# A fused attention, mixture-of-experts and rotation kernel: skew stores in six bundles, at most two scatters under way, and other places for some VectorE work

## The chip, the cores and the metric

The kernel runs on one core of a Trainium2 chip. The metric is the device time of one execution in microseconds (us); nine runs of the kernel before gave 685.74 to 692.51 us, median 689.94 us. All arithmetic is 32-bit floating point.

## The reference, cut to what matters

The input x has 4 batches of 512 tokens of 288 numbers. With a modulation computed from a condition vector, the reference computes, in this order:

```
h = ln(x) * (1 + scale) + shift                  # first half: attention
q, k, v = h @ w_qkv ; 16 heads of 18
x = x + gate * (softmax(q k^T / sqrt(18)) v @ w_proj)
xn = ln(x) * (1 + scale2) + shift2               # second half: experts
two of four experts per token, chosen by xn @ w_gate, gates by softmax
x = x + gate2 * sum(gate_e * (gelu(xn @ w1[e] + b1[e]) @ w2[e] + b2[e]))
v = silu(cond) @ W.T + b                         # 2016 numbers per batch
A = the 64x64 skew matrix with v above its diagonal and -v below ; R = expm(A)
U = Q of the QR factorization of P (288 x 64)
x = x + (z R - z) U^T   with z = x U
```

So beside the two large parts there are three small serial computations: the skew matrix and its exponential, the QR factorization (Householder, 64 columns one after the other), and the routing of tokens to experts.

## The kernel before, in words

The order of the work on each engine is written out by hand: each engine, and each DMA queue, executes its instructions strictly in the order in which the program issues them. What is said below of "before" and "behind" is this order.

**Attention.** 16 groups (4 batches b of 4 groups of four heads; group number n = 4b + g), each of four steps (128 keys each), so 64 steps, taken as 32 pairs numbered 0 to 31; a batch is 8 pairs, batch b begins at pair 8b. A step is `weigh`, that is 4 score matmuls (L1825) into a two-buffer PSUM tile z and two exponentials on ScalarE (L1834), and `gather`, 4 matmuls (L1845) of the exponentials with the values. The scores of a step can only be issued when the exponentials of the step before have emptied z. A pair p runs in this order:

1. `weigh(2p+1)`,
2. the pieces of its slot "a", then of slot "s",
3. one piece of the list `beside` (called "mid" below),
4. `weigh(2p+2)`, `gather(2p)`, `gather(2p+1)`; where a group ends: copy of its sums to oraw (ScalarE, L1864) and four small loads of the softmax denominators, den (L1867, SyncE's queue),
5. the pieces of slot "b", then another piece of `beside` (called "end"),
6. on GpSimd's queue: two stores that clear the slots, and up to five scatters.

The pieces that the change touches or moves things past:

- `reciprocals(n)` (slot "s"): VectorE inverts den (L1873), SyncE's queue stores it (rdr, L1875) and loads it back spread over the heads (spread, L1880). `divide(n)` (L1886, VectorE): oraw times spread. For group 3 of batch b these stand in pairs 8b+8 and 8b+9.
- `merge(b)` (pairs 8b+10 and 8b+11, slot "s"): four tiles of the output projection po (L1911), each of which reads all four oraw of the batch; VectorE adds po to xs (L1919) and takes its statistics (L1165).
- `begin(b+1)`: `first`, the layer norm's statistics of the next batch on VectorE (L1165, L1166) and four GpSimd operations behind them (L1178 to L1184); `norm`, four ScalarE activations with them (L1193), in slot "a" of pair 8b+2, so between the exponentials of two steps; `turns` and `values`, transposes and the value projection (L1214, L1736).
- `column` (L1585): one Householder column of the QR factorization, some 20 VectorE instructions that touch nothing else; 22 of them run in attention, the others in the expert part.
- `skew_matrices` (L1301): `product` (mid of pair 6) computes the 2016 numbers into four partition bands `row` of 504; `stores` writes them to a DRAM image of the matrices, one DMA for each run of a matrix row in a band, 66 in all; `load` reads the image, `last` transposes and subtracts. Four pieces of `stores` follow `product`, one for each band; the bands hold 9, 11, 14 and 32 runs.
- `rotations` (L1393): the exponential of A, 17 pieces called norm, levels, three powers, four Horner steps, turn, six squarings, last; `exponentials` puts empty pieces between them. TensorE does small products, VectorE the rest.
- `route` and `choose`: logits, top two, ranks, and at pair 23, slot "b", `slots_of`, the addresses where the tokens go. Then 16 scatters (L2178), one for 128 tokens and one choice, write the rows of the first half of the tokens into DRAM; up to five are issued at each pair's end. `slots_load` (pair 28) waits for all of them and loads the first expert's rows, xg (L2242 to L2249), on GpSimd's queue; TensorE transposes them in pairs 30 and 31 (L2293). The other 16 scatters follow in the expert part, one for each piece of expert work.

**Experts.** Eight expert halves one after the other: 36 weight tiles each for the hidden layer (L2531, L2544) and the output layer (L2591); the rest of the QR columns run on VectorE beside them. Then the rotation is applied and stored.

Of the kernel before, what the change touches and what calls it, by code (L numbers as in the profile page):

```python
# [20 lines left out]
HQ = 32  # L21
# [792 lines left out]
def fast_path(  # L814
# [24 lines left out]
    nc = tc.nc  # L839
    B, N, C = x.shape  # L840
# [4 lines left out]
    NG = w_qk.shape[2] // P  # L845
# [3 lines left out]
    D = pT.shape[0]  # L849
# [106 lines left out]
    with ExitStack() as s1:  # L956
# [344 lines left out]
        def skew_matrices(between):  # L1301

            width = NV // 4
            right.close()
            skew = right.enter_context(tc.tile_pool(name="skew", bufs=1, side="right"))
            um = skew.tile([2 * D, BH, D], F32, name="um")
            udr = dram.tile([D, B, D], F32, name="udr")
            wr = skew.tile([CC, NK, NV], F32, name="wr")  # L1310
            brs = skew.tile([P, width], F32, name="brs")
            row = brs

            def loads():
                nc.gpsimd.memset(um, 0.0)
                for h in range(2):
                    nc.gpsimd.dma_start(
                        out=udr[:, ts(h, BH), :], in_=um[ts(h, D), :, :]
                    )
                nc.gpsimd.memset(brs, 0.0)  # L1320
                for i in range(4):
                    nc.gpsimd.dma_start(
                        out=brs[i * HQ : i * HQ + B, :],
                        in_=br[ts(i, width)].partition_broadcast(B),
                    )
                for i in range(4):
                    nc.gpsimd.dma_start(
                        out=wr[:, :, ts(i, width)],
                        in_=wrT[:, ts(i, width)].rearrange("(k p) f -> p k f", p=CC),
                    )  # L1330

            def product():
                pa = bank([P, N], "pa")
                for k in range(NK):
                    for i in range(4):
                        nc.tensor.matmul(
                            pa[ts(i, HQ), :width],
                            scp[:, k, :],
                            wr[:, k, ts(i, width)],
                            start=(k == 0),  # L1340
                            stop=(k == NK - 1),
                        )
                nc.vector.tensor_add(row, pa[:, :width], brs)

            def stores(i, half):
                at, count = 0, 0
                for r in range(D - 1):
                    n = D - 1 - r
                    lo, hi = max(at, i * width), min(at + n, (i + 1) * width)
                    count += lo < hi  # L1350
                    if lo < hi and count % 2 == half:
                        nc.sync.dma_start(
                            out=udr[r, :, ds(r + 1 + lo - at, hi - lo)],
                            in_=row[i * HQ : i * HQ + B, ds(lo - i * width, hi - lo)],
                        )
                    at += n

            def load():
                for h in range(2):
                    nc.sync.dma_start(out=um[ts(h, D), :, :], in_=udr[:, ts(h, BH), :])  # L1360

            def last():
                pt = bank([P, N], "ptA")
                for b in range(BH):
                    for h in range(2):
                        at = ts(h, D)
                        nc.tensor.matmul(
                            pt[at, ts(b, D)],
                            um[at, b, :],
                            ident[at, at],  # L1370
                            start=True,
                            stop=True,
                        )
                nc.vector.tensor_sub(
                    A.rearrange("p b d -> p (b d)"),
                    um.rearrange("p b d -> p (b d)"),
                    pt[:, : BH * D],
                )
                right.close()

            idle = [lambda: None]
            return (
                [loads]
                + between
                + idle * 5
                + [product]
                + [lambda i=i: (stores(i, 0), stores(i, 1)) for i in range(4)]
                + [load]
                + idle * 5
                + [last]  # L1390
            )

# [569 lines left out]
        def choose(b, xr):  # L1962
# [190 lines left out]
            def slots_of():  # L2153
# [23 lines left out]
                def scatter(t, i):  # L2177
                    made = nc.gpsimd.indirect_dma_start(  # L2178
                        out=slots[h],
                        out_offset=bass.IndirectOffsetOnAxis(  # L2180
                            ap=where[:, i, t : t + 1], axis=0
                        ),
                        in_=xrs[t // NT][:, t % NT, :],
                        in_offset=None,
                        bounds_check=SLOTS - 1,
                        oob_is_err=False,
                    )
                    tc.declare_no_dep(
                        made.ins,
                        group=f"scatters{h}",  # L2190
                        reason="rows of one scatter are in no other",
                    )
                    tc.add_to_no_dep_group(f"scatters{h}", made.ins)
                    scattered[h].append(made.ins)

                scatters.extend(
# [111 lines left out]
        def exponentials():  # L2308
            pieces = []
            for i, piece in enumerate(rotations()):  # L2310
                pieces += [piece] + [lambda: None] * (3 if i == 0 else 1 + int(i == 1) if i < 11 else 0)
            pieces.pop(0)()
            beside[:0] = pieces[1:]

# [21 lines left out]
        def also(pair, slot, *pieces):  # L2336
            plan[pair][slot].extend(pieces)
# [7 lines left out]
        def divide(n):  # L2345
            ends_of[n][1]()
# [24 lines left out]
        for b in range(B):  # L2371
            at = b * HALF
            last = b == B - 1

            for p in {1: (0, 1, 6), 2: (0, 1, 7), 3: range(6)}.get(b, range(8)):
                also(at + p, "a", column)

            if b:
# [28 lines left out]
            for g in range(NG):  # L2407
                n = NG * b + g
                also_at = at + 2 * g + 2
                if also_at < PAIRS:  # L2410
                    also(also_at, "s", lambda n=n: reciprocals(n))
                    also(also_at + 1, "b", lambda n=n: divide(n))

            also(at + (4 if 0 < b < B - 1 else 6), "a", lambda b=b: residual(b))
            for p in {1: (3,), 2: (3,), 3: (6,)}.get(b, ()):
                also(at + p, "b", column)
            if not last:
                first, norm, turns, values = begin(b + 1)
                also(at + 1, "a" if b else "b", first)
                also(at + 2, "a" if b else "b", norm)  # L2420
                also(at + 3, "s", *turns)
                also(at + 4, "s", *values[:2])
# [501 lines left out]
```

## Time and profile before

The profiled execution took 689.83 us; the span of its instructions is 688.1 us, so 1.7 us lie around it.

| engine | busy us | share of the span |
|---|---|---|
| TensorE matmul (PE) | 660.6 | 96% |
| TensorE weight load (PEld) | 394.8 | 57% |
| VectorE (DVE) | 485.5 | 71% |
| ScalarE (ACT) | 294.5 | 43% |
| GpSimd (POOL) | 228.8 | 33% |

| part of the span | from us | to us |
|---|---|---|
| before the first exponential | 0 | 27.6 |
| attention, pairs 0 to 31 | 27.6 | 296 |
| experts and rotation | 296 | 688.1 |

How to read it: a line of the timeline gives start, duration, engine, source line, operation, the tiles written and read, and in brackets the idle time before it and what ended that. A line of the waits gives who waited for whom, the total, the number of times and the longest. A line of the stretches gives, for each engine, busy time and number of instructions, then the TensorE clock that was granted (1.00 is full speed), the DMA engines' busy share and GB/s. "SPq" is SyncE's queue. A matmul of 32-bit numbers shows as two records. A busy share of TensorE is not its peak: records of matmuls that follow each other slowly also look busy.

### The profile page before, as it was taken

The page shows a single profiled execution, that of the slowest core. Times are in us where ns is not written, and L with a number is a line of the kernel's source. Part 1 is how long each engine was busy: PE and PEld are TensorE (multiplying, and loading weights), DVE is VectorE, ACT ScalarE, POOL GpSimd, SP SyncE. Part 2 cuts the span into 40 slices and gives each one's busy share as a digit, 9 for nine tenths or more (in the row PEclk, how much of TensorE's full clock was granted, in tenths as well). Part 3 has the DMA queues.
Part 4 walks back from the last instruction along what each step waited for, and adds up shares of the span by engine and source line. Part 5 has one row for each costly group of instructions (what it writes and reads, how often), then busy time and mean ns, then how long its engine had stood idle before and what let it go on. Part 6 is the DMA issues. An engine that isn't in the chain of part 4 may idle for free. (4 is left out here: it accounts for less than half of the span.)

```text
span 688.1 us, 11454 instructions
## 1 busy us (share of the span) xinstructions
PE 660.6 (96%) x3563; PEld 394.8 (57%) x3563; DVE 485.5 (71%) x2207; ACT 294.5 (43%) x468; POOL 228.8 (33%) x352
## 2 busy tenths in 40 slices
PE   6999996999999999999999999999999999999995
PEld 5534333533353434356776767777677676776763
DVE  4554985397769888775996888888888887052135
ACT  4468564664566556751444223222232322312232
POOL 4034833415354277440431572304014032140110
PEclk9999998997999999999999999999999999999998
DMA  9457522212322124633631553344353053532035
GB/s 213 112 168 198 153 48 60 75 54 67 97 61 70 48 90 139 164 107 71 199 79 31 203 151 120 113 117 132 67 173 82 9 186 74 163 115 68 13 124 173
DMA packets 70624, 75.47 MB, mean 110 GB/s; under 512 B 33548, under 2 KB 57842, under 8 KB 70554
## 3 DMA queue, kind: packets, MB, share of 16 engines
q1 hardware_dynamic: 60166, 47.78, 25.7%
q0 software_dynamic: 9888, 26.45, 12.6%
q8 instruction: 30, 0.49, 0.3%
q10 hardware_dynamic: 500, 0.42, 0.3%
q14 instruction: 40, 0.33, 0.2%
HBM read 52.13 MB, written 18.23 MB: 102 GB/s over the span
## 5 line engine op out<-in xcount | busy, mean ns | idle before, releaser
L2591 PE MATMUL pe<-w2s,hm 128*128 128x288 f32 (+1 forms) x648 | 163.8, 408 | 0.0
L2531 PE MATMUL ph<-xgT,w1s 128*128 128x288 f32 (+2 forms) x576 | 151.7, 413 | 0.4
L1834 ACT ACTIVATE es<-z 128x1024 f32<-128x1024 f32 x128 | 126.2, 1022 | 58.1 <-PE z L1825 56.8
L2591 PEld LDWEIGHTS pe<-w2s,hm 128*128 128x128 f32 (+1 forms) x648 | 118.6, 187 | 32.0 <-issue 2.8
L2531 PEld LDWEIGHTS ph<-xgT,w1s 128*128 128x128 f32 x576 | 105.9, 190 | 40.2 <-issue 11.4
L2553 ACT ACTIVATE hm<-ph,b1r 128x576 f32<-128x576 f32 (+2 forms) x72 | 49.8, 737 | 132.5 <-PE ph L2544 132.5
L1825 PE MATMUL z<-qk 32*128 32x512 f32 x512 | 86.6, 648 | 1.3 <-ACT es L1834 1.3
L2606 POOL TENSOR_TENSOR y<-y,gb 128x288 f32<-128x288 f32 x32 | 27.7, 864 | 144.7 <-ACT y L2605 144.7
L1845 PE MATMUL av<-es,vt 128*32 128x512 f32 x512 | 62.3, 603 | 0.0
L2605 ACT ACTIVATE y<-pe,weight 128x288 f32<-128x288 f32 x32 | 16.0, 500 | 102.7 <-PE pe L2591 102.7
L1785 PE MATMUL pq<-hT,wqk 96*126 96x512 f32 (+3 forms) x120 | 55.7, 605 | 0.0
L2607 POOL DMA_INDIRECT chosen<-y,place x36 | 37.6, 1043 | 50.6 <-DVE y L2603 36.5
L1583 DVE SCALAR_TENSOR_TENSOR q<-q 64x1 f32<-64x1 f32 (+1 forms) x192 | 48.4, 252 | 6.9
L1825 PEld LDWEIGHTS z<-qk 32*128 32x128 f32 x512 | 28.6, 184 | 40.0 <-ACT es L1834 27.2
L2178 POOL DMA_INDIRECT slots<-xr,where x32 | 32.3, 1008 | 35.2 <-DVE where L2175 26.1
L1911 PE MATMUL po<-wpg,oraw 128*128 128x288 f32 x128 | 37.6, 442 | 6.6 <-POOL rs L1178 5.4
L1594 DVE STREAM_SHUFFLE wj<-pt 32x288 f32<-32x288 f32 (+47 forms) x96 | 42.1, 438 | 0.7
L1797 POOL DMA_DIRECT2D qk<-row x42 | 21.2, 513 | 58.2 <-ACT row L1792 57.9
L1785 PEld LDWEIGHTS pq<-hT,wqk 96*126 96x126 f32 (+3 forms) x120 | 20.4, 181 | 33.4 <-issue 30.2
L1845 PEld LDWEIGHTS av<-es,vt 128*32 128x32 f32 x512 | 13.6, 110 | 44.0 <-issue 44.0
L1911 PEld LDWEIGHTS po<-wpg,oraw 128*128 128x128 f32 x128 | 25.1, 204 | 21.2 <-issue 7.0
L1565 DVE SCALAR_TENSOR_TENSOR pt<-wj,uf,pt 64x288 f32<-64x288 f32 (+62 forms) x63 | 32.5, 515 | 2.2
(280 smaller groups left out, 869.1 us busy)
## 6 DMA issues: line engine op xcount, KB each, us to landing
w2s<-in_w_dram SPq DMA_DIRECT2D x8, 1296.0 KB
w1s<-in_w_dram SPq DMA_DIRECT2D x8, 1152.0 KB
slots<-empty POOLq DMA_DIRECT2D x36, 148.0 KB, 2.4
spread<-rdr SPq DMA_DIRECT2D x64, 64.0 KB
qk<-row POOLq DMA_DIRECT2D x42, 72.0 KB, 2.7
yc<-chosen SPq DMA_DIRECT2D x4, 576.0 KB
out_dram<-xs SPq DMA_DIRECT2D x8, 288.0 KB
wr<-in_wrT_dram POOLq DMA_DIRECT2D x4, 567.0 KB, 6.6
```

The source lines that it names most:

```text
L1565: nc.vector.scalar_tensor_tensor(m, w, u[rows, :], m, ALU.mult, ALU.add)
L1583: nc.vector.scalar_tensor_tensor(s, u, part, s, ALU.mult, ALU.add)
L1594: nc.vector.stream_shuffle(wj[o : o + HQ, j:], pt[o0 : o0 + HQ, j:], [j % HQ] * HQ)
L1785: nc.tensor.matmul(pq[:n], wqk[:rows, k, item, :n], hT[:rows, k, :], start=(k == 0), stop=(k == NK - 1),)
L1825: nc.tensor.matmul(zs[c // 2][:, c % 2, :], qk[ts(c, HQ), 1, ts(t, P)], qk[ts(c, HQ), 0, :], start=True, stop=True,)
L1834: nc.scalar.activation(e, z, AF.Exp, scale=SCALE)
L1845: nc.tensor.matmul(avs[n][ts(c, HQ), :], vts[b % 2][:, t, ds((4 * g + c) * (HD + 1), HQ)], es[c // 2][:, c % 2, :], start=(t == 0), stop=( ...
L1911: nc.tensor.matmul(po, oTs[NG * b + g][:, ts(t, P)], wpgs[b][:, g, :], start=(g == 0), stop=(g == NG - 1),)
L2531: nc.tensor.matmul(ph[:, j, :SB], w1s[:, k, ts(f, P)], xgT[:, k, ts(j, SB)], start=(k == 0), stop=False,)
L2553: nc.scalar.activation(hm[:, f, : CAPS[r]].rearrange("p (j s) -> p j s", j=NB), ph[:, :, :SB], AF.Gelu_apprx_tanh, bias=b1r[:, h, r, f : f ...
L2591: nc.tensor.matmul(po[ts(m, rows), :], slots_[:, f, :], w[:, f, :], start=(f == 0), stop=(f == NF - 1),)
L2607: nc.gpsimd.indirect_dma_start(out=chosen[h], out_offset=bass.IndirectOffsetOnAxis(ap=place[:, t : t + 1], axis=0), in_=y, in_offset=None, ...
```

## The change

- The 66 runs of the skew vector are put in one list in the order of the matrix's rows, and every sixth of it makes a bundle: six pieces of 11 stores in place of four of 9, 11, 14 and 32. One of the five empty pieces behind `load` goes, so `last` and the exponential's pieces come one piece (half a pair) later; one empty piece behind the first squaring goes too, so that from the second squaring on all stands where it stood.
- A scatter waits until the scatter two before it has landed. Before, no scatter waited for another.
- `divide` of a batch's last group moves from slot "b" to slot "s" of pair 8b+9.
- `column` moves from slot "a" to slot "b" in pairs 8, 9, 16, 17, 24 and 25.
- `first` of batches 2 and 3 moves from slot "a" to slot "b" of pairs 9 and 17, where it stands behind that pair's column.

```diff
-            def stores(i, half):
-                at, count = 0, 0
-                for r in range(D - 1):
-                    n = D - 1 - r
+            runs, at = [], 0
+            for r in range(D - 1):
+                n = D - 1 - r
+                for i in range(at // width, (at + n - 1) // width + 1):
                     lo, hi = max(at, i * width), min(at + n, (i + 1) * width)
-                    count += lo < hi
-                    if lo < hi and count % 2 == half:
-                        nc.sync.dma_start(
-                            out=udr[r, :, ds(r + 1 + lo - at, hi - lo)],
-                            in_=row[i * HQ : i * HQ + B, ds(lo - i * width, hi - lo)],
-                        )
-                    at += n
+                    runs.append((r, r + 1 + lo - at, i, lo - i * width, hi - lo))
+                at += n
+
+            def stores(part):
+                for r, to, i, lo, n in runs[part::6]:
+                    nc.sync.dma_start(
+                        out=udr[r, :, ds(to, n)],
+                        in_=row[i * HQ : i * HQ + B, ds(lo, n)],
+                    )
...
                 + [product]
-                + [lambda i=i: (stores(i, 0), stores(i, 1)) for i in range(4)]
+                + [lambda part=part: stores(part) for part in range(6)]
                 + [load]
-                + idle * 5
+                + idle * 4
                 + [last]
...
-                    tc.declare_no_dep(
-                        made.ins,
-                        group=f"scatters{h}",
-                        reason="rows of one scatter are in no other",
-                    )
-                    tc.add_to_no_dep_group(f"scatters{h}", made.ins)
+                    if scattered[h]:
+                        tc.declare_no_dep(
+                            made.ins,
+                            scattered[h][-1],
+                            reason="rows of one scatter are in no other",
+                        )
+                    if len(scattered[h]) > 1:
+                        tc.add_manual_dep(
+                            made.ins,
+                            scattered[h][-2].name,
+                            mybir.DependencyInfo(
+                                mybir.DependencyClass.Sync,
+                                mybir.DependencyReason.DATA,
+                            ),
+                            reason="two scatters at a time",
+                        )
...
-                pieces += [piece] + [lambda: None] * (3 if i == 0 else 1 + int(i == 1) if i < 11 else 0)
+                pieces += [piece] + [lambda: None] * (3 if i == 0 else 1 + int(i == 1) if i < 10 else 0)
...
-            for p in {1: (0, 1, 6), 2: (0, 1, 7), 3: range(6)}.get(b, range(8)):
+            for p in {1: (6,), 2: (7,), 3: range(2, 6)}.get(b, range(8)):
                 also(at + p, "a", column)
...
-                    also(also_at + 1, "b", lambda n=n: divide(n))
+                    also(also_at + 1, "s" if g == NG - 1 else "b", lambda n=n: divide(n))
...
-            for p in {1: (3,), 2: (3,), 3: (6,)}.get(b, ()):
+            for p in {1: (0, 1, 3), 2: (0, 1, 3), 3: (0, 1, 6)}.get(b, ()):
                 also(at + p, "b", column)
             if not last:
                 first, norm, turns, values = begin(b + 1)
-                also(at + 1, "a" if b else "b", first)
+                also(at + 1, "b", first)
                 also(at + 2, "a" if b else "b", norm)
```

## The prediction

> **What bounds the kernel now.** I read the page first: TensorE shows 96% busy, and from 296 us on every slice is full, so the experts pass on whatever attention gains or loses, one for one. The chain of waits covers only the last 24 us and names nothing here. So I looked at attention by stretches, one for each pair, and compared pairs of the same content in batches 1 and 2:
>
> ```profile
> core 0: us, PE busy (x) PEld busy (x) DVE busy (x) ACT busy (x) POOL busy (x), PEclk, DMA share, GB/s
> 105.60:124.20 18.60, 13.40 (x60) 7.55 (x56) 11.40 (x46) 6.58 (x9) 6.51 (x12) 0.82 0.22 63
> 186.20:197.00 10.80, 10.60 (x60) 5.70 (x58) 7.72 (x27) 6.59 (x9) 6.02 (x12) 1.00 0.21 59
> 213.20:222.10 8.90, 7.52 (x50) 2.68 (x46) 8.49 (x35) 4.49 (x5) 0.46 (x1) 1.00 0.22 66
> 156.00:168.10 12.10, 11.00 (x40) 5.68 (x44) 10.95 (x54) 4.80 (x7) 8.83 (x15) 0.62 0.30 93
> 229.70:239.70 10.00, 8.79 (x70) 4.73 (x66) 8.96 (x50) 4.72 (x6) 3.49 (x7) 1.00 0.31 81
> ```
>
> These are pairs 10, 18, 21, 15 and 23. Pair 10 costs 7.8 us more than its twin 18, pair 15 costs 2.1 more than 23, and both show a TensorE clock below 1. Then the waits of batch 1 (88.8 to 168.1 us):
>
> ```profile
> ACT xh L1193 <- POOL ms L1184: 6.9, 1, 6.9
> PE po L1911 <- POOL rs L1178: 5.2, 1, 5.2
> DVE den L1873 <- DMA udr<-brs: 4.4, 1, 4.4
> ACT g L2022 <- DVE g L2018: 3.5, 1, 3.5
> ```
>
> The second has a wrong name: `po` reads oraw, and `divide(3)` ended at 115.47 us, just before it resumed at 115.61. The queue of SyncE tells why `divide(3)` was late:
>
> ```profile
> 93.80 6.71 SPq L1352 DMA_DIRECT2D udr<-brs  x20
> 100.61 2.42 SPq L1867 DMA_DIRECT2D den<-oraw  x4
> 103.13 5.50 SPq L1352 DMA_DIRECT2D udr<-brs  x14
> 108.73 0.35 SPq L1875 DMA_DIRECT2D rdr<-den  x1
> 110.16 1.69 SPq L1880 DMA_DIRECT2D spread<-rdr  x4
> 111.95 10.76 SPq L1352 DMA_DIRECT2D udr<-brs  x32
> 124.33 1.14 SPq L1360 DMA_DIRECT2D um<-udr  x2
> 125.51 2.49 SPq L1867 DMA_DIRECT2D den<-oraw  x4
> ```
>
> The denominators stand behind skew stores at 0.336 us each. The clock, in two stretches:
>
> ```profile
> 115.60:121.30 5.70, 5.69 (x12) 4.13 (x13) 1.54 (x4) 2.18 (x4) 5.20 (x10) 0.50 0.20 53
> 158.90:169.10 10.20, 10.20 (x38) 5.29 (x40) 9.28 (x43) 3.30 (x5) 6.34 (x11) 0.50 0.29 93
> ```
>
> Half speed follows TensorE's idle 5.2 us (from 110.4, while `po` waited) and, the second time, an idle 1.35 us at 155.75.
>
> **The change part by part.** All sums are against the profiled 689.83 us (688.1 span, 1.7 around it), 0.11 below the median shown.
>
> *Stores.* The total stays 66 x 0.336 = 22 us of SyncE's queue. Ahead of group 3's den stand 22 stores in place of 20: den at 101.3, and den inverted 5.9 us later as before, at 107.1 (106.47 before). Behind it 11 in place of 14: the store of rdr no longer waits for the queue, spread goes out at 108.9 and lands 3.6 us later (as 130.88 to 134.46 did), at 112.5. The bundle of 32 becomes three of 11, with nothing between the first two and den of group 4 behind all: it goes out at about 121.6, not 125.51.
>
> *Columns, division, statistics in pairs 8 to 10.* Before, VectorE did column 8 (5.6 us) from 96.45 while den was on its way, and idled 4.4. After, it idles from 96.45 to 107.1, does column 8 (5.54) to 113.0, divides at once, and `po` resumes 0.83 us later, at 113.8: TensorE's wait is 3.4, not 5.2. But now column 9 stands ahead of the statistics: 113.7 + 5.5 + 2.34 = 121.6 (114.75 before). GpSimd's four operations take 2.55 more, ScalarE's norm 2.18: the exponentials of step 22 queued behind it start at 126.4, not 124.21. The next scores (step 23) need the first of them, 1.02 us: 127.5 against 125.90. **+1.6 us** for all of attention. The cover of the late statistics, TensorE's `po` until 123, is used up.
>
> *The clock after it.* TensorE has 4.6 us of `po` (18 records in pair 18), then 1.1 and 1.9 of scores and gathers, and idles from about 122 to 127.5. The bounds: no half speed, 0; half speed as after the 5.2 us, where those 18 records took 7.43 in place of 4.60 us, +2.8. The idle is nearest to that row: **+2.8**.
>
> [...]
>
> *Pairs 11 to 15.* Den of group 4 is inverted at about 126, not 129.17; its spread lands at 131.2. `divide(4)` then waits for the fourth `po` tile: 132.4 to 135 (134.46 before). From there to the top-two weights VectorE is full, 134.46 to 155.25 = 20.8 us: 153.2 to 155.8. ScalarE comes to `ratio` at 151.93 + 1.6 or + 4.4 = 153.5 or 156.3. So the wait of 3.5 us there goes, TensorE's 1.35, and the half speed behind them (the value projection took 6.13 us in place of 3.18 in pair 7). Late next: `levels`, now mid of pair 14 behind that pair's column. Its An, which the first power (end of pair 15) needs: weights + choices 1.1, divide 0.7, column 5.5, gates 1.0, reciprocals 0.45, levels 3.65 = 165.6 to 168.2. TensorE gets there at about 164 or 167. So the scores of step 33, at 170.34 before, come at 166.9 to 169.6: **-5.1** beside the +4.4, net -0.7 (-3.4 at full clock).
>
> *Pair 18.* Same reordering, statistics end at about 192.9 (190.35), norm at 197.6; the scores of step 39 came at 198.74 behind gathers, and the first exponential ends at 198.6: **0**, without slack; +0.5 if it slips.
>
> *Rotation pieces, half a pair later.* The third Horner product's wait for VectorE (1.38 us, pair 21) and the first squaring's (1.22, pair 23) go; `turn`, at the end of pair 22, waits for the last Horner step, which stands behind the top-two and a division: bounds -2.6 and 0, taken **-1.0**. Pieces from the second squaring on do not move. Columns 24 and 25 go behind small squarings that wait for nothing: 0; +0.4 if one squaring is late.
>
> *Scatters.* GpSimd is never idle over 0.31 us from `slots_of` to the last scatter, and the first expert's rows come right behind it:
>
> ```profile
> 273.48 0.97 POOL L2178 DMA_INDIRECT slots<-xr,where  x1 [0.31 <-issue]
> 276.64 0.95 POOL L2242 DMA_DIRECT2D xg<-slots  x1 [2.19 <-issue]
> 277.58 3.50 POOL L2245 DMA_DIRECT2D xg<-slots  x4
> ```
>
> These loads land 6.6 us (median) after issue, the last at about 287, and TensorE transposes them at 287.74: no slack. A scatter starts every 1.28 us and lands after 2.5/2.5/4.2 us (min, median, max), so the one two before has landed after 2.56: bounds 0 (no gain is possible, GpSimd's own cadence stays) and +1.6 for each landing of 4.2; taken +0.5, near the median. `slots_of` itself comes 0.5 earlier, the first squaring's VectorE work now being behind it. So the rows shift by -0.7 - 0.5 + 0.5, and the -1.0 above is lost to this wait: **+1.0**. In the expert part scatters are mostly one for each 4 to 5 us of work: 0; if one were late, the rows it delays are wanted tens of us later.
>
> **Sum:** +1.6 + 2.8 - 5.1 + 0 - 1.0 + 1.0 = -0.7: 689.1 for the profiled execution, 689.2 us for the median.
>
> **The rivals.**
>
> 1. *TensorE stays at full clock* behind the new wait of pair 10. For it: after idles of 1.38 and 1.22 us (220.5, 237.9) the clock stayed at 1.00. Against: 5.5 us resembles the 5.2. Then the scores of step 33 come 3.4 earlier and nothing else changes: 689.94 - 3.4 = 686.5; if the rows of the first expert also land earlier than the columns say, 685.5.
> 2. *Slower: the wait for `ratio` stays.* If VectorE does not get ahead in pairs 11 to 15 (den of group 4 still late, columns slowed by GpSimd's work, as column 14's 7.3 us was), the +4.4 of pairs 10 and 11 isn't given back: 694.3. It decides where `divide(4)` starts later than about 135.5, since 135.5 + 20.8 = 156.3 is ScalarE's arrival. For it: 132.4 to 135 is close. Against: three bundles of 11 free SyncE's queue 4 us earlier.
> 3. *Slower: scatters two at a time hold GpSimd.* If landings average 3.4 us where only two fly, each of the 14 waits costs 0.42, 6 us, all of it on the rows: 695. Against: nine landings of the eleven that can be read are under 3.1.
> 4. *The change doesn't act:* half speed and the waits of pairs 10 and 15 come as before, only a few tenths earlier or later: 689.9.
>
> **How the numbers follow.** The sum as it stands 0.40, rival 1 0.26, rival 2 0.21, rival 3 0.08, rival 4 0.05. Half a per cent is 3.45 us, about what a measurement of this kernel can tell (its nine runs spread over 6.8). Rival 1 gives a gain above it in most of its cases (0.22 of 0.26); the sum, own range 686.4 (full clock) to 692, in 0.05; so faster 0.27. Slower: rivals 2 and 3 nearly whole, 0.27, and 0.03 of the sum, should both unsure waits add: 0.30. Same: 0.43. The range reaches from rival 1's lower case less one (half speed in no place), 684.5, to rival 3's 695.
>
> **What would show it.** Right: SyncE's queue with 22 stores ahead of den and den of group 4 near 121.6; `divide(3)` near 113; ScalarE waiting for L1184 about 14 us in pair 10 (6.9 before), with step 22's exponentials near 126.4; the wait of `ratio` gone; the clock at half once between 122 and 136 and nowhere near 160; the transposes of xg waiting for a DMA. Wrong: step 22's exponentials before 124, the wait for `ratio` still at 3 us, GpSimd idle over 0.5 us before many scatters, or the experts' part (296 to 688) another length. What would upset the sum most is where half speed falls: two stretches in place of one cost 3 us more, none saves 3.

## The result, and the profile after

The changed kernel takes 700.51 us (median of 14 runs, 697.91 to 702.5) against 689.72 us (46 runs, 685.74 to 695.22): a ratio of 1.0158, 95% interval 1.0137 to 1.0179. It is slower by 1.6%. The prediction was 689.2 us and no change; the time lies above its range (684.5 to 695). The profiled execution took 702.29 us with a span of 700.6 (689.83 and 688.1 before). One group of four runs was disturbed: the kernel before took 707.36 us in it, and ScalarE stood idle for times that nothing in the traces accounts for; these four were run again, and the readings below are of the second runs.

A pair is measured here from the start of its first exponential to that of the next pair (pair 31 to the end of the last exponential), with the bounds rounded to 0.1 us. By pairs, after against before, in us:

| pairs | before | after | difference | predicted |
|---|---|---|---|---|
| to the start of pair 10 | 105.6 | 106.4 | +0.8 | 0 |
| 10, 11 | 26.4 | 30.5 | +4.1 | +4.4 |
| 12 to 15 | 36.0 | 38.1 | +2.1 | -5.1 |
| 16 to 20 | 45.0 | 42.8 | -2.2 | 0 |
| 21 to 24 | 36.9 | 41.8 | +4.9 | -1.0 |
| 25 to 29 | 34.6 | 34.6 | 0 | 0 |
| 30, 31 | 11.1 | 15.0 | +3.9 | +1.0 |
| the rest (experts) | 392.4 | 391.3 | -1.1 | 0 |

The stretches of the changed kernel that answer to those shown before, pairs 10, 18, 21, 15 and 23, then pair 30 (same columns: busy time of each engine with its instructions, then TensorE's clock):

```profile
core 0: us, PE busy (x) PEld busy (x) DVE busy (x) ACT busy (x) POOL busy (x), PEclk, DMA share, GB/s
106.40:126.30 19.90, 15.31 (x72) 7.88 (x64) 15.19 (x67) 6.53 (x10) 5.64 (x12) 0.83 0.16 45
191.90:202.30 10.40, 10.40 (x68) 5.83 (x64) 7.05 (x25) 6.62 (x10) 5.66 (x12) 1.00 0.29 89
217.80:224.90 7.10, 7.10 (x50) 2.60 (x46) 6.76 (x29) 4.50 (x6) 0.83 (x2) 1.00 0.22 75
159.10:174.90 15.80, 10.24 (x48) 4.46 (x47) 13.40 (x58) 4.76 (x6) 8.62 (x15) 0.79 0.30 89
233.50:248.00 14.50, 12.25 (x50) 6.68 (x50) 12.98 (x68) 4.65 (x7) 3.52 (x7) 0.60 0.22 56
294.30:304.00 9.70, 7.04 (x45) 2.53 (x41) 6.64 (x33) 5.67 (x9) 1.89 (x5) 0.86 0.51 105
```

Pair 15 (fourth row) has TensorE busy for 10.24 of 15.8 us, and pair 23 (fifth) is busy for 12.25 of 14.5 us, at a mean clock of 0.60. Pair 21 lost its wait, as predicted. TensorE's own lines show the new waits; the last bracket is the idle time before the instruction and what ended it:

```profile
114.40 7.58 PE L1913 MATMUL po<-wpg,oraw 128*128 128x288 f32 x18 [3.19 <-DVE oraw L1888]
...
127.29 2.13 PE L1827 MATMUL z<-qk 32*128 32x512 f32 x6 [2.39 <-ACT es L1836]
...
157.68 0.28 PE L1435 MATMUL pf<-fs,every 64*64 64x2 f32 x4
...
162.26 1.72 PE L1738 MATMUL pv<-wv,hT 97*128 97x288 f32 x6
169.54 3.25 PE L1738 MATMUL pv<-wv,hT 97*128 97x288 f32 x6 [5.56 <-DVE shrink L1440]
...
236.05 0.45 PE L1460 MATMUL pxt<-I,XY 64*64 64x64 f32 x8 [2.25 <-DVE XY L1498]
```

The first two are the waits of pair 10: the first as predicted (3.4 us), the second less than half as long (2.39 us for 5.5). The third is new: the value projection stops in its middle from 163.98 to 169.54. `levels` wrote its small product `pf` into one of the three rotating PSUM banks at 157.68, and VectorE copies it out only at 169.34. The last of the next three lines writes An, the scaled matrix that the first power needs:

```profile
164.47 2.62 DVE L1564 SCALAR_TENSOR_TENSOR prf<-pt,q,wj 64x278 f32<-64x278 f32 x1
...
169.34 0.15 DVE L1438 COPY norms<-pf 128x2 f32<-128x2 f32 x1
...
172.84 0.23 DVE L1453 TENSOR_SCALAR An<-pw 128x128 f32<-128x128 f32 x1
```

The column of pair 14 stands ahead of that copy and took 8.6 us (7.35 in the profile before), with one operation of it 2.62 us long in place of 0.5, while GpSimd multiplied `wpg` (164.49 to 167.74).

Four stretches ran wholly at half clock behind these waits, the last for 13.6 us:

```profile
113.60:120.40 6.80, 6.00 (x13) 4.32 (x14) 6.19 (x30) 0.00 (x0) 0.00 (x0) 0.50 0.02 2
127.25:134.00 6.75, 6.71 (x16) 3.73 (x17) 0.44 (x2) 2.84 (x3) 0.00 (x0) 0.50 0.30 69
168.25:175.00 6.75, 5.46 (x18) 2.57 (x22) 4.89 (x30) 0.47 (x2) 0.00 (x0) 0.50 0.15 41
236.50:250.10 13.60, 13.60 (x47) 6.71 (x50) 11.27 (x58) 4.02 (x6) 2.24 (x3) 0.50 0.17 46
```

SyncE's queue did what the prediction said: 22 stores, then the denominators at 100.48, 11 stores (102.95 to 107.58); those of group 4 behind 33 more, at 123.23 where 121.6 was predicted.

```profile
93.01 7.37 SPq L1355 DMA_DIRECT2D udr<-brs  x22
100.48 2.42 SPq L1869 DMA_DIRECT2D den<-oraw  x4
...
111.70 11.42 SPq L1355 DMA_DIRECT2D udr<-brs  x33
123.23 2.42 SPq L1869 DMA_DIRECT2D den<-oraw  x4
```

GpSimd's last scatters and the first expert's rows, in the changed kernel's timeline:

```profile
276.07 0.97 POOL L2180 DMA_INDIRECT slots<-xr,where  x1 [0.32 <-DMA slots<-xr,where]
277.56 1.15 POOL L2180 DMA_INDIRECT slots<-xr,where  x1 [0.52 <-DMA slots<-xr,where]
282.26 0.97 POOL L2180 DMA_INDIRECT slots<-xr,where  x1 [3.55 <-issue]
...
287.07 0.95 POOL L2254 DMA_DIRECT2D xg<-slots  x1 [2.56 <-PE po L1913]
```

From the first scatter (248.62) to this load are 38.5 us; before they were 33.0 (243.66 to 276.64). Of the 5.5 us, 3.25 are the stop ahead of the scatter at 282.26, the fifteenth of the 16 (3.55 us for the usual 0.30). It is no chance event: all eight profiles of kernels with the limit have a stop there, of 3.55 to 5.92 us, and none of the twelve profiles without it. The trace names nothing that GpSimd waits for in it.

### The profile page after: what moved, and what is told of

Same layout as the page of the kernel before. It is cut to its first block, busy times and chain, and to the rows that moved or that the text cites. A ratio compares the mean times of both kernels' runs of the same rounds, so it can differ in the third digit from the quotient of the medians.

```text
span 700.6 us, 11459 instructions
## 1 busy us (share of the span) xinstructions
PE 667.6 (95%) x3563; PEld 396.9 (57%) x3563; DVE 490.0 (70%) x2207; ACT 294.6 (42%) x468; POOL 227.9 (33%) x352
## 5 line engine op out<-in xcount | busy, mean ns | idle before, releaser
L1585 DVE SCALAR_TENSOR_TENSOR q<-q 64x1 f32<-64x1 f32 (+1 forms) x192 | 46.1, 240 | 6.9
L1913 PE MATMUL po<-wpg,oraw 128*128 128x288 f32 x128 | 39.2, 460 | 3.2 <-DVE oraw L1888 3.2
L1564 DVE SCALAR_TENSOR_TENSOR prf<-pt,q,wj 64x288 f32<-64x288 f32 (+62 forms) x63 | 34.5, 547 | 2.2
```

The source lines that it names most:

```text
L1564: nc.vector.scalar_tensor_tensor(pr[rows, :n], m, k, w, ALU.mult, ALU.mult, accum_out=u[rows, :])
L1585: nc.vector.scalar_tensor_tensor(s, u, part, s, ALU.mult, ALU.add)
L1913: nc.tensor.matmul(po, oTs[NG * b + g][:, ts(t, P)], wpgs[b][:, g, :], start=(g == 0), stop=(g == NG - 1),)
```

## The experiments

Three parts remain suspects beside the bundles: the shift of the rotation's pieces, the columns' and statistics' places, the scatter limit. Each was taken out of the changed kernel, and each was put alone into the kernel before. All ratios are to the kernel before on the same chip, with 95% intervals.

| kernel | ratio | interval |
|---|---|---|
| before + shift alone | 1.0081 | 1.0047 to 1.0116 |
| before + columns alone | 1.0132 | 1.0093 to 1.0172 |
| before + two scatters alone | 1.0098 | 1.0061 to 1.0134 |
| before + six bundles and division | 0.9998 | 0.9973 to 1.0024 |
| changed, all of them | 1.0158 | 1.0137 to 1.0179 |
| changed without the shift | 1.0144 | 1.0086 to 1.0202 |
| changed without the columns | 1.0119 | 1.0061 to 1.0176 |
| changed without the limit | 1.0155 | 1.0115 to 1.0195 |

**The shift taken out, and the shift alone.**

```
-                + idle * 4                    # behind the load, changed kernel
+                + idle * 3
-  ... 1 + int(i == 1) if i < 10 else 0)
+  ... 1 + int(i == 1) if i < 11 else 0)
```

> The changed kernel with the rotation's pieces half a pair earlier again, where they were before; the six bundles, the two scatters at a time and the new places of the columns stay. Theory A (the shift of the pieces costs most: levels holds the PSUM bank that the value projection of pair 15 wants, and turn waits for the last Horner step and brings half speed): pair 15 goes from 15.8 back to about 12, pairs 21 to 24 from 41.8 to about 37 us, so 700.5 - 3.7 - 4.9 = about 692. Theory B (the columns' new places make VectorE late, and whatever comes next in pairs 14 and 15 waits for it): pair 15 stays at 15 to 16, only pairs 21 to 24 change, 696 to 700.

> The changed kernel with the rotation's pieces back once more, since its first run held idle times of ScalarE that nothing in the trace accounts for. Theory A: no bank wait in pair 15 (7.9 us), no wait of turn in pairs 22 to 24, but the statistics of pair 18 now late (pair 18 14 to 15 us, as in the kernel with the columns alone) and the scatters' waits left: ratio 1.008 to 1.013. Theory B (nothing but the sum of parts): ratio 1.003 to 1.005.

The first run, in the disturbed group, gave 1.0018, the second 1.0144, more than theory A's 1.008 to 1.013. Pair 15 fell from 15.8 to 7.9 us in both, so the stall belongs to the shift, and theory B is out in both its forms. But pair 18 grew from 10.4 to 14.9 us, and pair 19 from 7.8 to 10.4: TensorE arrives early there and waits for an exponential that stands behind the late statistics. Pairs 25 and 26 took 19.0 us for 15.1, for a reason that the kernel with the columns alone shows below. In the second run:

```profile
199.43 2.13 PE L1827 MATMUL z<-qk 32*128 32x512 f32 x6 [3.85 <-ACT es L1836]
```

For the shift alone, the kernel before got `idle * 6` for `idle * 5` and `i < 10` for `i < 11`.

> The kernel before with only the rotation's pieces half a pair later (four bundles, all else as before). Theory A: the value projection of pair 15 waits for the bank that levels holds, +3, and turn brings 1.0 + 4.4 + 1.4 less the 1.9 of the Horner wait that goes, +4.9: 689.9 + 7 to 8 = 697 to 698. Theory B (the shift is harmless without the other parts): 688 to 691.

> The kernel before with the shift alone once more. Theory A: pair 15 15 to 16 us against 8 to 12 before, pair 21 7.1, pairs 22 to 24 30 to 35 us (28 before), ratio 1.008 to 1.012. Theory B: ratio 0.998 to 1.002.

Results 1.0158 (disturbed) and 1.0081, theory A's range. Pair 15 takes 15.8 us and pairs 22 to 24 34.6 us. The stall is there with the old places of the columns too:

```profile
166.09 3.25 PE L1736 MATMUL pv<-wv,hT 97*128 97x288 f32 x6 [5.78 <-DVE shrink L1438]
```

**The columns taken out, and alone.**

```
-            for p in {1: (6,), 2: (7,), 3: range(2, 6)}.get(b, range(8)):
+            for p in {1: (0, 1, 6), 2: (0, 1, 7), 3: range(6)}.get(b, range(8)):
-            for p in {1: (0, 1, 3), 2: (0, 1, 3), 3: (0, 1, 6)}.get(b, ()):
+            for p in {1: (3,), 2: (3,), 3: (6,)}.get(b, ()):
-                also(at + 1, "b", first)
+                also(at + 1, "a" if b else "b", first)
```

> The changed kernel with columns 8, 9, 16, 17, 24, 25 and the statistics' first part where they were before; the bundles, the last group's division, the shift and the scatter limit stay. Theory A: pairs 10 and 11 go from 30.5 back to about 26.4 us and the half speed at 127 goes, the wait for the ratio in pair 14 comes back in part (+1.8 at most), pair 15 keeps its stall: 700.5 - 4.1 + 1 = about 697.5. Theory B (the columns' places are the cause of the stall in pair 15 too): 693 to 694.

> The changed kernel with the columns and the statistics back once more. Theory A: pairs 10 and 11 25 to 26 us (30.5 in the changed kernel), pair 15 still 15 to 16.5 with the value projection waiting 5 us or more for VectorE, pair 30 9 to 14 us from the scatters: ratio 1.008 to 1.013. Theory B (the columns cause the stall of pair 15): pair 15 8 to 12 us and ratio 1.003 or less.

Results 0.9933 (disturbed) and 1.0119. The half speed near 127 is gone and pair 11 takes 7.8 us for 10.6 (pairs 10 and 11 together 27.2); pair 15 keeps its stall (16.5 us, a wait of 6.2 us), against theory B. Pair 30 takes 13.6 us in this profile.

The same edit the other way round, on the kernel before:

> The kernel before with the new places of columns 8, 9, 16, 17, 24, 25 and of the statistics' first part alone. Theory A: pairs 10 and 11 30 to 31 us (26.4 before) with half speed near 127, ratio 1.003 to 1.006, less if the ratio's wait of pair 14 shrinks. Theory B (harmless without the other parts): 26 to 27 us and ratio 0.999 to 1.001.

1.0132, more than either theory gave. Pairs 10 and 11 take 30.7 us, as expected. The rest was not: this kernel has no stall in pair 15 (7.9 us), so it comes to pair 18 early and pays there, with the next batch's statistics ending at 195.3 where the prediction had 192.9:

```profile
200.50 2.98 PE L1825 MATMUL z<-qk 32*128 32x512 f32 x8 [3.75 <-ACT es L1834]
```

Pair 18 takes 14.8 us and pair 19 10.5 (10.8 and 8.3 before). The prediction's "0, without slack" for pair 18 holds only while something else makes attention late. The same is true of its 0 for the columns of pairs 24 and 25. Here a column stands ahead of the copies that a squaring needs, one operation of it takes 3.25 us in place of 0.43 beside GpSimd's multiplication of `wpg`, TensorE waits 1.98 us for the squaring, and half speed follows from 264.25: pairs 25 and 26 take 18.8 us for 15.1. The changed kernel without the shift has the same wait there (2.25 us).

```profile
254.91 3.25 DVE L1604 SCALAR_TENSOR_TENSOR sq<-wj 64x272 f32<-64x272 f32 x1
262.80 0.68 PE L1458 MATMUL psq<-XY 64*64 64x64 f32 x16 [1.98 <-DVE XY L1510]
```

**The scatter limit taken out, and alone.** The changed kernel with the group of the kernel before (all scatters of a half free of each other); the other way round, the two dependencies of the change put into the kernel before.

> The changed kernel with the scatters of a half free of each other, as before; all else stays. Theory A (waits between scatters make the first expert's rows late): from the first scatter to the first load of rows 33 us instead of 38.5, pair 30 from 9.7 back to about 6.2, the total 697. Rival C (the rows are late because all of attention was late, and VectorE's own work at the end holds pair 30): pair 30 stays near 9.7 and the total at 700.5.

> The changed kernel with free scatters once more, because in its first run ScalarE stood still 12.8 and 2.8 us for nothing that the trace names, in the experts and near 279 us. Theory A: pair 30 6 to 7 us and 3.5 us under the changed kernel, ratio to the kernel before 1.010 to 1.012. Rival C: pair 30 near 9.7, ratio 1.015 to 1.017.

Results 1.0186 (disturbed) and 1.0155, as rival C said. From first scatter to first load are 34.8 us, but pair 30 stays at 9.1 us, since VectorE's addition of the last `po` tiles, which the profile names as what the transposes wait for, is as late as the rows were:

```profile
297.69 0.55 PE L2295 MATMUL pt<-ident,xg 128*128 128x128 f32 x3 [2.50 <-DVE xs L1921]
```

> The kernel before with at most two scatters under way, all else as before. Theory A (GpSimd waits for landings and the first expert's rows are late by it): first scatter to first load of rows 37 to 38.5 us (33.0 before), pair 30 9 to 10 us (6.2 before), ratio 1.004 to 1.006. Rival C (the late rows came from the late attention): 33 to 34 us, pair 30 6 to 7 us, ratio 0.999 to 1.002.

1.0098: theory A, and larger than it said. 42.9 us lie between first scatter and first load, 9.9 more than before: 3.7 of them are again the stop ahead of the fifteenth scatter, 2.25 one wait for a scatter that landed after 4.57 us. Pair 30 takes 14.3 us:

```profile
272.44 1.14 POOL L2178 DMA_INDIRECT slots<-xr,where  x1 [2.55 <-DMA slots<-xr,where]
278.82 0.97 POOL L2178 DMA_INDIRECT slots<-xr,where  x1 [3.96 <-issue]
...
292.06 0.66 PE L2303 MATMUL pt<-ident,xg 128*128 128x128 f32 x2 [5.20 <-DMA xg<-slots]
294.20 1.73 PE L2303 MATMUL pt<-ident,xg 128*128 128x128 f32 x7 [1.47 <-DMA xg<-slots]
```

So in the changed kernel two waits end nearly together in pair 30 (its transposes wait 0.85 us for the rows and 1.81 for VectorE), and taking one away gives little.

**Six bundles and the division alone.** On the kernel before, the new `stores` with six entries and `idle * 3` behind the load, and the division in slot "s".

> The kernel before with the six bundles (the idle entries behind them cut so that the rotation's pieces keep their places) and the last group's division in slot s: no shift, no new places of columns, no limit on scatters. Theory A (the shift and the columns' places are what costs; the bundles themselves are a gain, since den of group 4 goes out 4 us earlier and VectorE gets ahead of ScalarE's ratio): pairs 10 and 11 25.4 us (26.4 before), the ratio's wait in pair 14 2 us or less, no bank wait in pair 15: pairs 14 and 15 16 to 18 us (21.2 before), in all 4 to 6 us under the kernel before of the same chip (ratio 0.992 to 0.994). Theory D (the bundles make no difference by themselves): ratio 0.998 to 1.002.

Ratio 0.9998. The local forecast came true, the total did not. Pairs 14, 15 and 18 of this kernel:

```profile
145.20:153.00 7.80, 7.80 (x50) 2.59 (x49) 7.25 (x39) 4.96 (x7) 0.00 (x0) 1.00 0.16 36
153.00:160.80 7.80, 7.80 (x52) 3.71 (x48) 7.13 (x38) 4.70 (x7) 7.38 (x14) 1.00 0.47 144
179.60:194.00 14.40, 12.28 (x60) 6.78 (x56) 9.53 (x37) 6.58 (x10) 6.47 (x12) 0.88 0.25 73
```

Pairs 14 and 15 are full and at full clock, 15.6 us for 21.2. Pair 18 then costs 3.6 us more than before (TensorE waits 2.12 us for the division of group 7, which stands behind a column and the statistics; half speed follows), and near 310 `po` of the last group waits 2.4 us (1.2 before), with half speed behind it.

**Which resource holds pair 15.** In the changed kernel, the copy that frees the bank on ScalarE:

```
-                nc.vector.tensor_copy(norms[:, :BH], pf[:, :BH])
+                nc.scalar.copy(norms[:, :BH], pf[:, :BH])
```

> The changed kernel with one instruction moved to another engine: the copy of the norms out of PSUM, the first thing of levels, goes from VectorE to ScalarE, which is free at that point of its order; VectorE keeps everything else of levels. Theory A (the value projection of pair 15 waits for the PSUM bank, not for An): TensorE no longer idles 5 us before the value projection, no half speed near 168; the first power may now wait 1 to 3 us for An; pair 15 9 to 12 us (15.8 in the changed kernel); the lead is lost in part at pair 18, whose statistics then come late: ratio 1.008 to 1.014. Rival E (VectorE's own lateness is what counts, and An is as late as the bank): the wait moves to the first power at its full length, pair 15 14 to 16 us, ratio 1.015 to 1.017.

1.0166, rival E in the total and in the wait. The value projection no longer waits and pair 15 itself takes 7.5 us, less than either theory said; the next in line, the first power, waits for An instead, and half speed behind it makes pair 16 18.6 us long:

```profile
173.12 0.69 PE L1460 MATMUL pw<-pw,An 64*64 64x64 f32 x8 [4.57 <-DVE An L1453]
```

The bank was the first thing to be late, not the only one: VectorE as a whole gets to `levels` 11.7 us after TensorE (169.34 against 157.68 in the changed kernel).

**turn half a pair later**, in the changed kernel (the first squaring keeps its place):

```
-  (3 if i == 0 else 1 + int(i == 1) if i < 10 else 0)
+  (3 if i == 0 else 1 + int(i in (1, 8)) if i < 9 else 0)
```

> The changed kernel with turn half a pair later, directly ahead of the first squaring, which keeps its place. Theory A (the wait of 2.25 us of turn for the last Horner step brings the half speed of 13.65 us, and most of the 4.9 us of pairs 21 to 24 are that): wait gone or under 1 us, full clock from 236 to 250, pairs 22 to 24 27 to 30 us (34.7 in the changed kernel), ratio 1.007 to 1.011. Rival F (the wait goes along with turn to the first squaring, which needs Y at once): 1.5 to 2.5 us of wait at pair 23 and 33 to 35 us, ratio 1.014 to 1.017.

1.0176. The wait stays at full length, now behind the expert choices, and half speed lasts only 3.4 us in this profile; pairs 22 to 24 take 31.8 us, and yet the median is not better. The spell of 13.65 us is thus not a fixed price of that wait, and what makes it long stays open.

```profile
241.25 0.69 PE L1460 MATMUL pxt<-I,XY 64*64 64x64 f32 x8 [2.66 <-DVE pos L2081]
```

**The bundles later on SyncE's queue.** The kernel with six bundles and the division, with idle entries between `product` and the bundles: two of them (and one behind the load), then one (two behind), then two with the load and the transposes of the skew matrices two entries later as well (three behind, and `1 if i == 0` for `3 if i == 0`).

> The kernel before with the six bundles, the last group's division in slot s, and the bundles two entries later, so that on SyncE's queue the denominators of group 3 go out ahead of all stores and those of group 4 ahead of 22. If SyncE's queue is what holds pair 10 (den of group 3 was copied at 91 us and issued at 100.6 behind 20 stores): den of group 3 issued near 93, division near 108 in place of 115, po's wait of 5.2 us and the half speed behind it gone, pair 10 11 to 12 us; of the 7 us some are lost again at pair 18 if VectorE paces attention there: ratio 0.988 to 0.995. If VectorE's columns hold pair 10 instead: division at 113 or later and ratio 0.997 to 1.001.

1.0044. Denominators of group 3 out at 91.4, pair 10 10.4 us (18.6 before), no wait of `po`: the queue is what held pair 10. But the load of the skew matrices is now late, and pair 12 takes 17.5 us for 7.7, with half speed behind the wait:

```profile
131.60 1.25 PE L1369 MATMUL ptA<-ident,um 64*64 64x64 f32 x8 [5.96 <-DMA um<-udr]
```

> The kernel before with six bundles, the division in slot s and the bundles one entry later (one bundle ahead of the denominators of group 3, three more ahead of those of group 4, the load of the skew matrices near 124): division 3 at 108 to 110, pair 10 10.5 to 12 us, no wait for the skew matrices in pair 12, pair 16 beginning at 154 to 157 (168.1 before). If TensorE carries that to the end: ratio 0.985 to 0.99. If VectorE and the DMA round trips of the denominators pace attention (what was gained by pair 16 was lost again at pair 18 and near 310 in the kernels with six bundles): ratio 0.995 to 1.001.

1.0021 (0.9991 to 1.0050): pair 10 takes 10.4 us, pair 12 waits 3.8 us for the same load and has 13.65 us at half speed near 137. The profiled execution also lost 5.8 us in pair 8, behind a wait of 2.48 us for VectorE that began before the first bundle went out and that the other profiles of these kernels don't have.

> As the kernel with the stores two entries later, and the transposes of the skew matrices two entries later too, with levels in its old place: pair 10 10.4 us, no wait of 6 us for the load in pair 12 and no half speed at 129 behind it, pair 16 beginning at 153 to 156. Carried to the end: ratio 0.985 to 0.99. Paced by VectorE and the denominators' round trips: ratio 0.995 to 1.001.

0.9976 (0.9946 to 1.0006). Pair 16 begins at 165.3, not at 153 to 156: in pair 14 `levels` waits 4.1 us for VectorE.

> The same kernel as f4 again, beside it on the same chip: ratio 0.995 to 1.000; a ratio of 1.000 or more means that its first result was the spread of the runs.

0.9994 (0.9972 to 1.0016): no difference. Its SyncE queue near the end of attention (store of the last denominators, then their spread):

```profile
299.77 0.42 SPq L930 DMA_DIRECT2D w2s<-in_w_dram  x1
300.80 0.34 SPq L1878 DMA_DIRECT2D rdr<-den  x1
306.24 1.71 SPq L1883 DMA_DIRECT2D spread<-rdr  x4
```

**The load of second weights behind that spread:**

```
-        weights2 = [expert_weights2(0)]
+        weights2 = []
...
-            both_(lambda: reciprocals(NN - 1), third_[0]),
+            both_(lambda: reciprocals(NN - 1),
+                  lambda: weights2.append(expert_weights2(0)), third_[0]),
```

> As the kernel with stores and skew transposes two entries later, and the load of the first expert's second weights (1296 KB) issued behind the spread of the last group's denominators in place of ahead of it. If the end of attention is held by that spread (stored at 300.96, issued only at 306.0, 5 us later where others took 1.4 to 3.1; division 15 at about 310 whatever attention gained before): the spread is issued 1.4 to 2 us after the store, division 15 about 3 us earlier, po no longer waits 2.6 us near 310; 2.5 to 3 us under f4, ratio to the kernel before 0.992 to 0.995. If not: the ratio of f4, 0.997 to 1.000.

685.22 us, ratio 0.9935 (0.9912 to 0.9959), 3.8 us under its neighbour without this edit: faster than both kernels. The spread follows its store after 1.4 us in place of 5.4, the last division ends at 304.3, where it was 310.3 (2.8 of the 6.0 us are there at the store already), and `po` does not wait there:

```profile
298.04 0.35 SPq L1878 DMA_DIRECT2D rdr<-den  x1
299.48 1.71 SPq L1883 DMA_DIRECT2D spread<-rdr  x4
301.70 0.41 SPq L930 DMA_DIRECT2D w2s<-in_w_dram  x1
```

What is left in it is the wait of `levels` in pair 14, 4.49 us, with 10.24 us at half clock behind it. This load was not moved alone, in the kernel before.

## Why the prediction was wrong

- **Stores, columns, statistics in pairs 8 to 11: right; the clock there in part by luck.** `divide(3)` at 113.56 (113 predicted; it waited 2.16 us for its spread, and not for the column ahead of it), `po` waiting 3.19 us (3.4), ScalarE waiting 12.9 us for L1184 (14), its norm ending and the exponentials starting at 126.24 (126.4), half speed from 127.2 (between 122 and 136), +4.1 us (+4.4). But the half speed was taken over from an idle of 5.2 us for one of 5.5, and the idle was 2.39: the sum had `po` at full speed, and it ran at half from 113.6, a second spell that the prediction didn't have. In the changed kernel without the scatter limit, which is the same program up to there, `po` did not wait, the idle was 5.36, half speed came once, and pairs 10 and 11 took 27.2 us in place of 30.5.
- **Pairs 11 to 15 (12 to 15 in the table), -5.1 predicted, +2.1 measured: the step that failed most.** The wait for the ratio shrank as foreseen (3.5 to 1.17). Wrong was "Its An ... 165.6 to 168.2. TensorE gets there at about 164 or 167": An came at 173.07. The terms of that sum which were mis-sized are the columns: that of pair 11 took 8.1 us where its time in the trace before was 6.7, and that of pair 14 8.6 where 5.5 were taken, although rival 2 quotes 7.3 for it from the trace before; together 4.5 of the 4.9 us by which An missed the upper bound. `divide(4)` started at 135.61, just past rival 2's bound of 135.5. And TensorE needed VectorE earlier than the step says: `pf` holds a bank from 157.68, which the value projection of pair 15 wants, ahead of the first power. A moved step was followed to its next reader, but not to the next user of its buffer. The experiment with the copy on ScalarE shows that the bank alone did not decide: An was 4.57 us late for the first power anyway.
- **The half speed of pair 15 counted as a gain that could be had.** The -5.1 held the 3 us of half speed at 158.9 in the profile before. In the kernel with the two scatters alone, which is the kernel before up to 243 us, the same wait (1.37 us; 1.34 before) stands at the same place with no half speed, and pair 15 takes 7.8 us in place of 12.1: a price from one execution that another execution doesn't pay.
- **Pair 18, 0 predicted:** in the changed kernel right only because the stall of pair 15 came first; +4.0 us wherever nothing has stalled TensorE in pairs 15 and 16 and the columns are moved (the columns alone, the changed kernel without the shift). The same two kernels lose 3.7 and 3.9 us in pairs 25 and 26, where the prediction had 0 for the columns behind the squarings.
- **Rotation pieces, -1.0 predicted, +4.9 measured.** The wait of the third Horner product went (-1.9 in pair 21), and `turn` waits 2.25 us, near the upper bound named for it. The clock behind that wait was left out: `turn` was weighed as a wait alone, while the wait of pair 10 had been given its half speed.
- **Scatters, +0.5 predicted, with +1.0 for the rows in all; +3.9 measured in pairs 30 and 31.** The limit moved the rows by 5.5 us, and alone it costs 6.9 us between the medians, which is the price of rival 3, given 0.08. Its mechanism was only a part of it: landings had a median of 2.6 us and not 3.4, and the waits for them come to some 1.6 us; the larger part, 3.25 us, is the stop ahead of the fifteenth scatter, which the prediction didn't have and whose cause stays open. In the changed kernel itself the limit costs nothing that can be measured (1.0155 without it): VectorE's addition of the last `po` tiles is as late, and that the prediction had at nothing.
- **That the parts add.** Alone they cost 0.81, 1.32 and 0.98%, 3.1% together if they added; the changed kernel loses 1.58%, and 1.2 to 1.55% with any one of them taken out. The time gained by one part is waited for elsewhere: the six bundles bring pair 16 forward by 7.3 us and the total by nothing. That VectorE's order, with the round trips of the denominators in it, sets the end from pair 8 to 19 as much as TensorE's does is a reading, not shown by an experiment. For it speaks that VectorE's idle time between 88 and 200 us hardly changes: 34.6 us in the kernel before, 33.9 with the six bundles, 36.1 after the change and 34.7 with the bundles and the load later, whatever TensorE waits for.

Rival 1 (full clock in pair 10) and rival 4 (nothing acts) did not hold in the profile after. Rival 2 ended on the right side, and its condition held in part (columns slowed beside GpSimd's work), but the delay fell elsewhere: the wait for the ratio, on which it rests, was two thirds gone, and `levels` was late instead.

## What to carry to other kernels

When a piece is moved, look at who next needs its buffer (here a PSUM bank taken by a product of 2 columns), not only at who needs its result; and give every wait that the move makes the same clock risk. Before a local gain is added to the total, ask which later wait it runs into. Here the denominators of group 3 earlier on the queue took 8.2 us out of pair 10 and left the total where it was; it fell by 0.65% only when the 1296 KB load was out of the way of the last ones too.

## What the runs showed of the hardware

**The spells of half clock lie on a grid of 3.41 us windows.** In the 16 profiles outside the disturbed group the spells of half clock begin at multiples of 3.413 us from each other (after the change at 113.59, 127.24, 168.20, 236.47 and 301.32, that is 0, 4, 16, 36 and 55 windows; before it at 114.51 and 158.88, 13 windows apart), and but for the one cut off by the end of a span they last whole windows. The grid lies elsewhere in each execution (counted from the start of the span, by 0.92 us in these two). Cut each on its own grid, from the first exponential to the last window that another whole one follows, they give 2,983 windows at full clock: where TensorE's recorded matmuls fill less than 42% of a window, the next ran at half in 48 of 48 cases; above 61%, in none of 2,896; between, in 10 of 39. The kernel before and the changed kernel have 370 of these windows: 7 of 7, none of 362, 1 of 1. Two windows that hold the same wait, in the kernel before and in the one with two scatters alone:

```profile
155.47:158.88 3.41, 2.06 (x12) 0.60 (x8) 3.01 (x21) 3.01 (x5) 2.47 (x5) 1.00 0.23 51
```

```profile
155.21:158.62 3.41, 2.04 (x16) 0.43 (x8) 3.01 (x21) 2.46 (x4) 1.49 (x3) 1.00 0.10 20
```

Both are busy for 60%; the first was followed by half clock, the second was not. The waits of 2.25 and 2.39 us in the changed kernel, which but for 0.05 us of the second lie each in one window, were followed by half clock; a wait of 3.60 us in the kernel with the shift alone (111.06 to 114.66), of which at most 1.89 lie in one window, was not. The two rows above hold waits of 1.34 and 1.37 us; of the 20 windows busy for 58 to 61%, 3 were followed by half clock.

**One VectorE operation took five times as long beside GpSimd.** L1564 took 2.62 us in the column of pair 14; GpSimd's four `tensor_tensor` of L1904 ran at 164.49 to 167.74. In the 20 profiles the same operation, at its widths of 257 to 288 on 64 partitions, took 0.48 to 0.55 us in the 600 cases where no tensor operation of GpSimd overlapped it, and 0.48 to 2.73 us in the 40 where one did (0.49 in the kernel before; 0.48, 2.62 and 2.73 in the changed kernel).

**ScalarE stood still for 8 to 14 us** with nothing in the trace that released it: once or twice in each of the four profiles of the disturbed group (8.0 us at the shortest, 13.69 with the shift alone, where TensorE waited 9.0 us for it), and in none of the other 16. What held it was not found.
